# Turning x to stand by token: TensorE transposes against ScalarE block copies and VectorE 32 by 32 transposes

## The chip, the cores and the metric

The kernel runs on one core of a Trainium2 chip. The metric is the device time of one execution in microseconds (us). All arithmetic is fp32. The engines are TensorE (PE in the profile; its weight loads are PEld), VectorE (DVE), ScalarE (ACT), GpSimd (POOL) and SyncE (SP), which issues all the DMAs that matter here. Each engine runs its own instructions strictly in their order; semaphores tie the engines together.

## The reference

One layer over 2048 tokens with 1024 channels. The input is normalized per token (layernorm); the result is the input, plus a Mamba-2 block of the normalized input, plus a LoRA mixture of experts of the normalized input. Cut to the part around the change:

```
proj = hidden @ in_proj_w.T                  # gate (4096) | x (4096), B (1024), C (1024) | dt (64)
xBC  = silu(conv4(x, B, C))                  # a causal convolution of 4 taps per channel
dt_p = softplus(dt + dt_bias);  dA = exp(-dt_p * exp(A_log))
state_t = state_{t-1} * dA_t + (dt_p_t * x_t) outer B_t     # 64 heads of 64 channels, 128 states
y_t     = state_t . C_t + D * x_t
out     = (rmsnorm(y) * silu(gate)) @ out_proj_w.T
```

The recurrence is computed in chunks of 128 tokens. In a chunk, y is one matmul of a masked 128 by 128 matrix per head with `dt*x`, and the state takes one matmul of `decay*dt*x` with B. Both need `dt*x` with the tokens on the partitions, while the convolution leaves x with the channels on the partitions. So each chunk of x has to be turned.

## The kernel before

**Stages.** The projections of x, B and C (and two eighths of the gate) are made by products of 128-row weight tiles with 512-column operands (`pair`, L499), seven products of four matmuls for each two by two block of tiles (a Strassen scheme; `left_operands`, L462, makes its weight sums on GpSimd). Results go to DRAM as `raw`. The scan works on 32 blocks (L1056): two halves s of the tokens, eight groups g of 512 channels, and two halves of 512 tokens each. A block has four chunks of 128 tokens, so there are 128 slots in all (the two loops at L1087 and L1091). The later stages (gate, output projection) are not changed.

**One slot.** The slot of chunk c has, in program order: one product from the stream of projections; `scan_b` of chunk c (L812); a part of `scan_a` of the next chunk (L748); a second product; a part of `scan_a`; a third product (and a fourth in some slots); the last part of `scan_a`. `products` (L655) issues one product and then the steps of side work in that part's list: `conv` (L692) of the next block, layernorm steps, norm squares, weight sums.

`scan_a` has three parts. The first scans the decays on VectorE (`es`, L757). The second makes C by B and B transposed on TensorE into one PSUM bank (L765, L766), copies them out on ScalarE (`cbm`, `bt`, L769, L771), puts D times x into the PSUM bank of y (L778) and masks on VectorE (`dab`, L783). The third is where the change lies: four TensorE transposes of the chunk's x into the PSUM bank `st` (L788 to L790), eight ScalarE scalings by dt into `xdt` (L795, one for each head), and eight more by the decay into `xdd` (L803).

`scan_b` has eight matmuls of `xdt` and `dab` into y (L828), four of the state with C (`ps_e`, L834), two VectorE instructions that finish y (L841, L842), one matmul of `xdd` with `bt` for the state (`ps_st`, L846) and its addition (L856).

**What sets the order.** Nothing is ordered by hand for every instruction: a scheduler places them. Instructions that are passed to `keep_in_program_order` (all matmuls, the `xdt` and `xdd` scalings, the silus, the squares) keep their order on their engine; VectorE instructions passed to `pin` (L98) are chained; the rest is placed where the scheduler thinks it is ready. PSUM banks `aux`, `y`, `e` and `st` have one buffer each.

Of the kernel before, what the change touches and what calls it, by code (L numbers as in the profile page):

```python
# [8 lines left out]
F32 = mybir.dt.float32  # L9
# [34 lines left out]
def mamba_lora_kernel(  # L44
# [85 lines left out]
    def load_piece(s, i, tag, pool):  # L130

        t = pool.tile([P, KT, 2, Q], F32, tag=tag, name=f"piece_{s}_{i}")
        if s == 0:
            for h in range(2):
                nc.sync.dma_start(
                    t[:, 4 * h : 4 * h + 4].rearrange("p k n q -> p k (n q)"),
                    x_view[:, 4 * h : 4 * h + 4, i * 2 * Q : (i + 1) * 2 * Q],
                )
        else:
            for n in range(2):  # L140
                at = s * TS + n * TB + i * Q
                nc.sync.dma_start(t[:, :, n, :], x_view[:, :, at : at + Q])
        piece_of[s, i] = t
# [5 lines left out]
    for m in range(2):  # L149
        for k in range(2):  # L150
            what = f"a{m + 1}{k + 1}"
            first_w[what] = wp.tile([P, KH, P], F32, tag="w", name=f"{what}_x0_0")
            nc.sync.dma_start(first_w[what], w_in[32 + m, :, k * KH : (k + 1) * KH, :])
    load_piece(0, 2, "xg", p2)
    load_piece(0, 3, "xg", p2)

    wsm = lp.tile([P, KT, NSM], F32, name="wsm")
    nc.sync.dma_start(wsm, w_small)
# [17 lines left out]
    def op_tile(j, name):  # L176
        return op.tile([P, KH, TB], F32, tag=f"op{j}", name=name)

    ops_of["x", 0] = [op_tile(j, f"op_{j}_0") for j in range(7)]
    xop_d = [  # L180
        [dram.tile([P, KH, TB], F32, tag=f"xop_{s}_{j}", name=f"xop_{s}_{j}") for j in range(7)]
        for s in range(NS)
# [80 lines left out]
    def first_sums():  # L263


        b11, b21, b22, t4, t1, t2, b12 = ops_of["x", 0]
        nc.vector.tensor_tensor(t1, b12, b11, ALU.subtract)
        nc.vector.tensor_tensor(t2, b22, t1, ALU.subtract)
        nc.vector.tensor_tensor(t4, b21, t2, ALU.subtract)
        nc.vector.tensor_tensor(b12, b22, b12, ALU.subtract)  # L270
# [60 lines left out]
    def small(s, i, chunks, sm, home):  # L331
# [65 lines left out]

        for c in range(nch):
            nc.vector.tensor_tensor_scan(
                run[:, c, :], da[:, c, :], zero, 1.0, ALU.mult, ALU.add  # L400
            )


# [318 lines left out]
        yield  # L722


    mid_of = {}
    masked = []
    decay_of = {}
# [20 lines left out]
    def scan_a(s, g, half, c):  # L748

        key = s, g, half, c  # L750
        n = f"{s}_{g}_{half}_{c}"
        dab, ecp = decay_of.pop(key)
        hs = slice(g * HG, (g + 1) * HG)
        cs = slice(c * Q, (c + 1) * Q)

        es = p1.tile([P, HG, Q], F32, tag="es", name=f"es_{n}")
        ins = nc.vector.tensor_tensor_scan(  # L757
            es.rearrange("p h t -> p (h t)"), dab.rearrange("p h t -> p (h t)"), here, 0.0,
            ALU.mult, ALU.add,
        )  # L760
        pin(ins)
        yield
        xg, bc = xbc_of[s, g, half]
        psm = ps_one.tile([P, 3, Q], F32, tag="aux", name=f"ps_cb_{n}")
        mm(psm[:, 0, :], bc[:, 0, cs], bc[:, 1, cs], start=True, stop=True)  # L765
        transpose(psm[:, 1, :], bc[:, 0, cs])  # L766
        put_sums = norm_sum(psm[:, 2, 0:2]) if squares else None
        cbm = p2.tile([P, Q], F32, tag="cbm", name=f"cbm_{n}")
        nc.scalar.copy(cbm, psm[:, 0, :])  # L769
        bt = p2.tile([P, Q], F32, tag="bt", name=f"bt_{n}")  # L770
        nc.scalar.copy(bt, psm[:, 1, :])  # L771
        if put_sums:
            put_sums()

        psy = ps_one.tile([P, 4, Q], F32, tag="y", name=f"ps_y_{n}")
        for j in range(4):
            at = 4 * g + j
            nc.scalar.activation(  # L778
                psy[:, j, :], xg[:, j, cs], AF.Copy, scale=dsk[:, at : at + 1]
            )  # L780
        ms = dab
        masked[:] = [
            nc.vector.tensor_tensor(  # L783
                ms, es, cbm.unsqueeze(1).to_broadcast([P, HG, Q]), ALU.mult
            )
        ]
        yield
        pst = ps_one.tile([P, 4, Q], F32, tag="st", name=f"ps_xt_{n}")  # L788
        for j in range(4):
            transpose(pst[:, j, :], xg[:, j, cs])  # L790
        xdt = p2.tile([P, HG, HP], F32, tag="xdt", name=f"xdt_{n}")
        x_t = pst.rearrange("p j (a q) -> p (j a) q", q=HP)
        for h in range(HG):
            at = g * HG + h
            ins = nc.scalar.activation(  # L795
                xdt[:, h, :], x_t[:, h, :], AF.Copy,
                scale=dt_of[s][:, half * NQ + c, at : at + 1],
            )
            tc.keep_in_program_order(ins)

        xdd = p1.tile([P, HG, HP], F32, tag="xdd", name=f"xdd_{n}")
        for h in range(HG):
            ins = nc.scalar.activation(  # L803
                xdd[:, h, :], xdt[:, h, :], AF.Copy, scale=es[:, h, Q - 1 : Q]
            )
            tc.keep_in_program_order(ins)
        mid_of[key] = ms, ecp, bt, xdt, xdd, psy
        yield
# [149 lines left out]
    def out_sums(pool, i):  # L958

        p, q, kt = i // 8, i // 4 % 2, i % 4  # L960
        t = pool.tile([P, 7, 4, P], F32, tag="wo", name=f"wo_{i}")
        x = pool.tile([P, 7, P], F32, tag="wox", name=f"wox_{i}")

        def store(j, src):
            nc.sync.dma_start(w2_d[p][:, j, :, q, kt, :].rearrange("i c o -> c i o"), src)

        for j, (m, k) in enumerate(((0, 0), (0, 1), (1, 1), (1, 0))):
            nc.sync.dma_start(
                t[:, j].rearrange("c (m k) o -> c m k o", m=2),
                w_out[4 * p + 2 * k : 4 * p + 2 * k + 2, 2 * q + m, :, :, kt, :]  # L970
                .rearrange("k c m o -> c m k o"),
            )
        yield

        add(t[:, 5], t[:, 0], t[:, 3], ALU.subtract)
        add(t[:, 3], t[:, 3], t[:, 2], ALU.add)
        add(t[:, 4], t[:, 3], t[:, 0], ALU.subtract)
        add(t[:, 6], t[:, 1], t[:, 4], ALU.subtract)
        yield
        store(0, t[:, :, 0])  # L980
        store(1, t[:, :, 1])
        store(3, t[:, :, 3])
        yield
        t0, t1, t2, t3 = (t[:, :, k] for k in range(4))
        add_in_slot(x, t0, t2, ALU.subtract)
        add_in_slot(t2, t2, t3, ALU.add)
        add_in_slot(t0, t2, t0, ALU.subtract)
        add_in_slot(t1, t1, t0, ALU.subtract)
        yield
        store(6, x)  # L990
        store(4, t2)
        store(5, t0)
        store(2, t1)
        yield
# [3 lines left out]

    for h in range(HG):
        nc.gpsimd.tensor_copy(here[:, h * Q : (h + 1) * Q], ident)  # L1000
    zero = lp.tile([H, Q], F32, name="zero")
    nc.gpsimd.memset(zero, 0.0)

    rank = lp.tile([P, NE], F32, name="rank")
# [3 lines left out]
    nc.vector.tensor_scalar(na, na, -1.0, None, ALU.mult)  # L1008

    lns = [ln_first(i) for i in range(NQ)]  # L1010
    sm0 = p1.tile([P, 2 * NQ, NSM], F32, tag="y", name="sm_0")

    def small_first(i):
        for c in range(2 * i, 2 * i + 2):
# [46 lines left out]
    for part in range(3):  # L1061
        load_raw(*blocks[1], part)
    load_decays(*blocks[0], 1)

    ps = ps_one.tile([P, 4 * Q], F32, tag="y", name="ps_clear")
    mm(ps, ident, here[:, 0 : 4 * Q], start=True, stop=True)
# [20 lines left out]
    for b, blk in enumerate(blocks):  # L1087
# [3 lines left out]
        for c in range(NQ):  # L1091
# [34 lines left out]
            if nxt:  # L1126
# [5 lines left out]
                if c < 3:  # L1132
                    parts[1] += steps(conv_steps, 1)
                    parts[2] += steps(conv_steps, 1)

            products(1, parts[0])
            scan_b(*blk, c)
            if b == 16 and c == 1:
# [679 lines left out]
```

## Time and profile before

| what | value |
|---|---|
| median of 3 runs | 3382.65 us (3381.43 to 3383.46) |
| the profiled execution | 3379.91 us |
| its span on the core | 3378.1 us |
| TensorE busy | 3337.6 us, 99% of the span |
| VectorE busy | 2412.2 us, 71% |
| ScalarE busy | 1460.3 us, 43% |
| GpSimd busy | 688.3 us, 20% |
| first and last transposes of x (`ps_xt`) start | 174.6 and 2071.8 us |
| granted TensorE clock over the span | 0.998 |

How to read it: the profile is of one execution, whose own time (3379.91 us) is 2.74 us under the median of the runs; its span is 1.81 us shorter than its time. The page counts an engine as busy while an instruction of it is open, overlaps counted once, so instructions that overlap show a mean duration longer than their busy share. A group's row gives line, engine, operation, output and input, shape, count, busy us, mean ns of one, then the idle time of the engine just before such instructions and what ended it. In a timeline a row of several instructions gives the start of the first and the stretch to the end of the last. On TensorE an fp32 matmul shows as two records, a transpose as one.

### The profile page before, as it was taken

To read this page: it belongs to the slowest core of one execution; us is meant where nothing else is said; L and a number is where in the kernel's file an instruction comes from. 1 tells how busy PE (TensorE), PEld (TensorE's weight loads), DVE (VectorE), ACT (ScalarE), POOL (GpSimd) and SP (SyncE) were. 2 spreads that over 40 slices of the span, in tenths; PEclk is the share of its full clock that TensorE was granted. 3 is DMA by queue.
4 is the path that set the end of the run, shared out by engine and by line. 5 is a ranking of instruction groups with operands and counts; after the bars stand their busy time and mean duration, and the time that the engine had idled before them with its cause. 6 is when DMAs were issued, how large, how long until landed. Compare 5 with 4: busy or idle time off the path is not lost.

```text
span 3378.1 us, 41773 instructions
## 1 busy us (share of the span) xinstructions
PE 3337.6 (99%) x14021; PEld 2197.4 (65%) x14021; DVE 2412.2 (71%) x2745; ACT 1460.3 (43%) x4018; POOL 688.3 (20%) x483
## 2 busy tenths in 40 slices
PE   9999999999999999999999999999999899999999
PEld 8455555555555555555555555788888788888888
DVE  7478787878768787877787784577877666556654
ACT  2266666766665666565666663222222100000000
POOL 4122222222100021212121212355544100000000
PEclk9999999999999999999999999999999999999999
DMA  7556666656689989998888889578777886585644
GB/s 255 191 174 221 203 200 198 225 186 207 208 305 312 331 257 309 279 298 255 269 260 268 261 284 298 174 264 284 254 265 262 286 305 234 204 299 182 211 168 144
DMA packets 550821, 826.75 MB, mean 245 GB/s; under 512 B 36688, under 2 KB 266320, under 8 KB 547024
## 3 DMA queue, kind: packets, MB, share of 16 engines
q1 hardware_dynamic: 550608, 824.08, 74.0%
q8 instruction: 112, 1.84, 0.2%
q14 instruction: 101, 0.83, 0.1%
HBM read 564.88 MB, written 259.06 MB: 244 GB/s over the span
## 4 chain that ended last, share of the span: by engine, by line
PE 92%; DVE 3%; DMA 2%; ACT 2%; issue 1%; SPq 0%; DVEq 0%; ACTq 0%
PE ps_x_x L81 13%; PE ps_a_x L81 9%; PE ps_x_w L81 8%; PE ps_y_x L81 8%; PE ps_x_z L81 6%; PE ps_a_w L81 6%; PE ps_y_w L81 6%; PE ps_a_z L81 4%; PE ps_y_z L81 4%; PE ps_e L81 4%; PE ps_y L81 3%; PE ps_st L81 3%; PE ps_x_b L81 2%; PE ps_x_g L81 2%; PE ps_a_b L81 2%; PE ps_y_g L81 2%
## 5 line engine op out<-in xcount | busy, mean ns | idle before, releaser
L715 DVE SCALAR_TENSOR_TENSOR xg<-raw_x,cw,xg 128x512 f32<-128x512 f32 x384 | 344.6, 901 | 11.9 <-ACT xg L708 5.9
L85 POOL TENSOR_TENSOR state<-state,tot 128x512 f32<-128x512 f32 x112 | 120.7, 1078 | 1111.7 <-PE ps_e L81 1012.1
L81 PE MATMUL ps_x_w<-t,w 128*128 128x256 f32 x1344 | 304.3, 379 | 1.4 <-DVE kept L1719 0.8
L757 DVE TENSOR_TENSOR_SCAN es<-dab,here 128x1024 f32<-128x1024 f32 x128 | 296.1, 2313 | 9.1 <-ACT xdd L803 6.4
L81 PEld LDWEIGHTS ps_x_w<-t,w 128*128 128x128 f32 x1344 | 255.6, 190 | 44.3 <-issue 8.8
L803 ACT ACTIVATE xdd<-xdt,es 128x64 f32<-128x64 f32 x1024 | 262.4, 391 | 0.0
L778 ACT ACTIVATE ps_y<-xg,dsk 128x128 f32<-128x128 f32 x512 | 190.2, 371 | 164.7 <-DVE xg L842 150.6
L795 ACT ACTIVATE xdt<-ps_xt,dt 128x64 f32<-128x64 f32 x1024 | 223.8, 335 | 68.2 <-PE ps_xt L116 68.0
L841 DVE TENSOR_TENSOR ecp<-ecp,ps_e 128x512 f32<-128x512 f32 x120 | 82.2, 685 | 225.9 <-PE ps_e L81 207.7
L81 PE MATMUL ps_a_w<-q,w 128*128 128x256 f32 x896 | 202.6, 379 | 1.6 <-DMA w<-w 1.6
L1755 ACT COPY ps_x_w<-ps_a_w 128x512 f32<-128x512 f32 x28 | 16.0, 570 | 417.3 <-PE ps_a_w L81 417.3
L81 PEld LDWEIGHTS ps_a_w<-q,w 128*128 128x128 f32 x896 | 170.2, 190 | 25.1 <-DMA w<-w 2.0
L783 DVE TENSOR_TENSOR dab<-es,cbm 128x1024 f32<-128x1024 f32 x128 | 161.1, 1258 | 30.1 <-ACT cbm L769 29.6
L81 PEld LDWEIGHTS ps_y<-dab,xdt 128*64 128x64 f32 x2048 | 111.3, 136 | 103.5 <-ACT xdd L803 90.1
L81 PE MATMUL ps_x_x<-op_again,s_x 128*128 128x512 f32 x384 | 173.8, 595 | 0.7 <-ACT s_x L531 0.7
L81 PE MATMUL ps_a_x<-op_again,a_x 128*128 128x512 f32 x384 | 173.2, 594 | 0.0
L81 PE MATMUL ps_y_x<-op_again,s_x 128*128 128x512 f32 x384 | 173.1, 593 | 0.0
L715 DVE SCALAR_TENSOR_TENSOR bc<-raw_b,cw,bc 128x512 f32<-128x512 f32 x192 | 159.1, 830 | 18.5 <-ACT bc L708 14.6
L81 PE MATMUL ps_x_x<-op,s_x 128*128 128x512 f32 x368 | 166.2, 594 | 0.5 <-ACT s_x L531 0.5
L81 PE MATMUL ps_y_x<-op,s_x 128*128 128x512 f32 x368 | 165.9, 593 | 0.0
L81 PE MATMUL ps_a_x<-op,a_x 128*128 128x512 f32 x368 | 165.8, 593 | 0.0
L476 POOL TENSOR_TENSOR s_x<-a_x,a_x 128x512 f32<-128x512 f32 x48 | 74.8, 1559 | 362.1 <-PE ps_y_x L81 227.5
(327 smaller groups left out, 6631.8 us busy)
## 6 DMA issues: line engine op xcount, KB each, us to landing
w<-w SPq DMA_DIRECT2D x196, 512.0 KB, 3.9
dab<-da_d SPq DMA_DIRECT2D x128, 512.0 KB, 6.0
raw<-ev SPq DMA_DIRECT2D x192, 256.0 KB, 3.7
a_x<-in_w_in_dram SPq DMA_DIRECT2D x168, 256.0 KB, 4.5
w<-wo SPq DMA_DIRECT2D x96, 448.0 KB, 5.0
ecp<-run_d SPq DMA_DIRECT2D x256, 128.0 KB, 5.0
y<-xg SPq DMA_DIRECT2D x64, 512.0 KB, 5.5
gy<-y SPq DMA_DIRECT2D x64, 512.0 KB, 6.6
```

The costliest lines, as they stand in the source:

```text
L81: tc.keep_in_program_order(nc.tensor.matmul(*args, **kw))
L85: ins = nc.gpsimd.tensor_tensor(*args)
L476: nc.gpsimd.tensor_tensor(t[what], t[x], t[y], alu)
L715: ins = nc.vector.scalar_tensor_tensor(dst[:, i, :], raw[:, i, k : k + TB], cw[:, ti, k : k + 1], dst[:, i, :], ALU.mult, ALU.add,)
L757: ins = nc.vector.tensor_tensor_scan(es.rearrange("p h t -> p (h t)"), dab.rearrange("p h t -> p (h t)"), here, 0.0, ALU.mult, ALU.add,)
L778: nc.scalar.activation(psy[:, j, :], xg[:, j, cs], AF.Copy, scale=dsk[:, at : at + 1])
L783: nc.vector.tensor_tensor(ms, es, cbm.unsqueeze(1).to_broadcast([P, HG, Q]), ALU.mult)
L795: ins = nc.scalar.activation(xdt[:, h, :], x_t[:, h, :], AF.Copy, scale=dt_of[s][:, half * NQ + c, at : at + 1],)
L803: ins = nc.scalar.activation(xdd[:, h, :], xdt[:, h, :], AF.Copy, scale=es[:, h, Q - 1 : Q])
L841: pin(nc.vector.tensor_tensor(ecp, ecp, pse, ALU.mult))
L1755: nc.scalar.copy(px, pa)
```

## The change

x of a block is turned by a new generator `turned`, for two chunks (256 tokens) at a time. Sixteen ScalarE copies move 32-partition runs: run i of the channels, token block b goes to the partitions of run b, at place i (256 elements on 32 partitions each). Then one VectorE transpose of 128 by 1024 elements turns every 32 by 32 block in place. The result `x_by_token` holds two chunks and is read by the `xdt` scalings from SBUF, where they read PSUM before. The four TensorE transposes of each chunk are gone. The copies are kept in program order, the VectorE transpose is in the pinned chain. In the loop, the steps of `turned` are laid into the parts of the slots: ten in the slots of c = 2 and c = 0, seven in those of c = 3 and c = 1, the last of the seven being the transpose; the first seventeen steps of block 0 stand ahead of the loop.

The other edits: the pieces 2 and 3 of the input at the start lie in the places of two operand tiles, which are made only in `first_sums`; the early small projections (`sm0`) take a buffer of `xg`; the constant zero of a scan is one column, broadcast; and `out_sums` makes its differences in place, in another order, without the tile `wox`.

```diff
-    load_piece(0, 2, "xg", p2)
-    load_piece(0, 3, "xg", p2)
+    load_piece(0, 2, "op3", op)
+    load_piece(0, 3, "op4", op)
...
-    ops_of["x", 0] = [op_tile(j, f"op_{j}_0") for j in range(7)]
+    ops_of["x", 0] = [None if j in (3, 4) else op_tile(j, f"op_{j}_0") for j in range(7)]
...
     def first_sums():
+        for j in (3, 4):
+            ops_of["x", 0][j] = op_tile(j, f"op_{j}_0")
...
-                run[:, c, :], da[:, c, :], zero, 1.0, ALU.mult, ALU.add
+                run[:, c, :], da[:, c, :], zero.to_broadcast([H, Q]), 1.0, ALU.mult, ALU.add
...
+    by_token = {}
+
+    def turned(s, g, half):
+
+        if not by_token:
+            by_token["x"] = p1.tile([P, 2, 4 * P], F32, tag="xT", name="x_by_token")
+            by_token["in"] = p1.tile([P, 2, 4, 4, 32], F32, tag="xin", name="x_blocks")
+        xT, blocks = by_token["x"], by_token["in"]
+        x = xbc_of[s, g, half][0].rearrange("p j (c b r) -> p j c b r", c=NQ, b=4)
+        for k in range(2):
+            for i in range(4):
+                for b in range(4):
+                    ins = nc.scalar.copy(
+                        blocks[32 * b : 32 * b + 32, :, :, i, :].rearrange("p c j r -> p j c r"),
+                        x[32 * i : 32 * i + 32, :, 2 * k : 2 * k + 2, b, :],
+                    )
+                    tc.keep_in_program_order(ins)
+                    yield
+            ins = nc.vector.transpose(
+                xT.rearrange("p c x -> p (c x)"),
+                blocks.rearrange("p c j i r -> p (c j i r)"),
+            )
+            pin(ins)
+            yield
...
-        pst = ps_one.tile([P, 4, Q], F32, tag="st", name=f"ps_xt_{n}")
-        for j in range(4):
-            transpose(pst[:, j, :], xg[:, j, cs])
         xdt = p2.tile([P, HG, HP], F32, tag="xdt", name=f"xdt_{n}")
-        x_t = pst.rearrange("p j (a q) -> p (j a) q", q=HP)
+        x_t = by_token["x"][:, c % 2, :].rearrange("p (h q) -> p h q", q=HP)
...
-        x = pool.tile([P, 7, P], F32, tag="wox", name=f"wox_{i}")
...
-        add_in_slot(x, t0, t2, ALU.subtract)
-        add_in_slot(t2, t2, t3, ALU.add)
-        add_in_slot(t0, t2, t0, ALU.subtract)
+        add_in_slot(t3, t2, t3, ALU.add)
+        add_in_slot(t2, t0, t2, ALU.subtract)
+        add_in_slot(t0, t3, t0, ALU.subtract)
         add_in_slot(t1, t1, t0, ALU.subtract)
         yield
-        store(6, x)
-        store(4, t2)
+        store(6, t2)
+        store(4, t3)
...
-    zero = lp.tile([H, Q], F32, name="zero")
+    zero = lp.tile([H, 1], F32, name="zero")
...
-    sm0 = p1.tile([P, 2 * NQ, NSM], F32, tag="y", name="sm_0")
+    sm0 = p2.tile([P, 2 * NQ, NSM], F32, tag="xg", name="sm_0")
...
     load_decays(*blocks[0], 1)
+    turn = turned(*blocks[0])
+    for _ in range(17):
+        next(turn)
...
+            if c == 2 and nxt:
+                turn = turned(*nxt)
+            if c < 2 or nxt:
+                for p, k in zip(parts, ((2, 3, 3, 2), (3, 4), (0, 3, 4, 3), (3, 4))[c]):
+                    p += steps(turn, k)
```

## The prediction

> **What bounds the kernel now.** I read the page's busy shares first, then the stretch of the scan by windows, then the groups by shape, TensorE's waits, and one slot's timeline.
>
> ```profile
> PE 3337.6 (99%) x14021; PEld 2197.4 (65%) x14021; DVE 2412.2 (71%) x2745; ACT 1460.3 (43%) x4018; POOL 688.3 (20%) x483
> ```
> ```profile
> 200.00:2000.00 1800.00, 1786.82 (x7314) 952.17 (x7313) 1424.52 (x1719) 1138.18 (x3401) 348.72 (x250) 1.00 0.79 251
> ```
>
> The second line is the scan stage (PE, PEld, DVE, ACT, POOL). TensorE is the bound there, idle for 13 of 1800 us at full clock; VectorE is busy 79% and ScalarE 63%. Some 123 of the 128 slots lie in it, so a slot lasts 14.7 us, of which ScalarE works 9.3 and VectorE 11.6.
>
> ```profile
> L116 PE MATMUL ps_xt<-ident,xg 128*128 128x128 f32 x512 | 76.8, 273 | 0.0
> ```
> ```profile
> L803 ACT ACTIVATE xdd<-xdt,es 128x64 f32<-128x64 f32 x1024 | 262.4, 391 | 0.0
> L795 ACT ACTIVATE xdt<-ps_xt,dt 128x64 f32<-128x64 f32 x1024 | 223.8, 335 | 68.2 <-PE ps_xt L116 68.0
> ```
> ```profile
> L757 DVE TENSOR_TENSOR_SCAN es<-dab,here 128x1024 f32<-128x1024 f32 x128 | 296.1, 2313 | 9.1 <-ACT xdd L803 6.4 <-DMA raw<-ev 2.4 <-DMA dab<-da_d 0.4
> L783 DVE TENSOR_TENSOR dab<-es,cbm 128x1024 f32<-128x1024 f32 x128 | 161.1, 1258 | 30.1 <-ACT cbm L769 29.6
> ```
> ```profile
> PE ps_st L81 <- ACT xdd L803: 4.8, 10, 1.4
> ...
> PE ps_y L81 <- ACT xdt L795: 4.6, 3, 1.6
> ```
>
> The first is what goes. The next two are the ScalarE scalings that use its result; the two after are the VectorE rows nearest to the new transpose. The last two are TensorE's waits for the scalings: small today. How much room there is behind them is the question, and one slot's timeline shows it, TensorE first, then ScalarE:
>
> ```profile
> 729.33 0.60 PE L116 MATMUL ps_xt<-ident,xg 128*128 128x128 f32 x4
> 729.77 3.60 PE L81 MATMUL ps_y_g<-op,s_g 128*128 128x512 f32 x8
> 733.30 1.09 PE L81 MATMUL ps_y<-dab,xdt 128*64 128x128 f32 x16
> 734.32 1.16 PE L81 MATMUL ps_e<-bc,state 128*128 128x128 f32 x8
> 735.32 1.02 PE L81 MATMUL ps_st<-xdd,bt 128*128 128x512 f32 x2
> ```
> ```profile
> 726.26 0.26 ACT L769 COPY cbm<-ps_cb 128x128 f32<-128x128 f32 x1
> 726.40 0.28 ACT L771 COPY bt<-ps_cb 128x128 f32<-128x128 f32 x1
> 729.53 0.57 ACT L523 COPY ps_x_g<-ps_a_g 128x512 f32<-128x512 f32 x1 [2.84 <-PE ps_a_g L81]
> 730.01 1.06 ACT L879 ACTIVATE sq<-xg 128x1024 f32<-128x1024 f32 x1
> 730.97 1.75 ACT L795 ACTIVATE xdt<-ps_xt,dt 128x64 f32<-128x64 f32 x8
> 732.55 2.05 ACT L803 ACTIVATE xdd<-xdt,es 128x64 f32<-128x64 f32 x8
> ```
>
> Here xdd ends at 734.60 and `ps_st`, which needs all of it, starts at 735.32: 0.7 us to spare with a square (0.96) ahead of xdt, about 1.7 without.
>
> **What goes.** The four transposes start at 729.33 and the next product at 729.77: 0.44 us for four, 0.11 each, though each row says 273 ns (they overlap). 128 slots make **-56 us**, all on the path, since TensorE is never ahead of its inputs for long.
>
> The Trainium skill ("VectorE: DVE Perf Modes", The three transpose paths and Rules for kernel authors) speaks against this change: it would have a full 128 by 128 transposed on TensorE, VectorE's being blocks of 32 only. But it puts TensorE's at 390 ns each (bf16); by that 512 would give back an estimated 200 us, and the sum would be clearly faster. The trace's pace of 0.11 us decides.
>
> **What ScalarE takes on.** 32 copies for each of 32 blocks, 1024 of 256 elements from SBUF. No such row stands in the trace. Start to start, a copy of 128 columns takes 0.14 us (726.26 to 726.40), one of 512 takes 0.48 (729.53 to 730.01): 0.25 at 256 on that line, from PSUM. From SBUF the square of 1024 takes 0.96 (730.01 to 730.97), which less 768 columns at the same slope (0.34/384) is 0.28. The far end is xdd, 64 columns from SBUF in 0.24, plus 192 at that slope: 0.41, but with a scale read from memory, which a copy lacks. So between 0.25 and 0.41; I take **0.31**, near the copies. Eight per slot are 2.5 us. xdt now reads SBUF, so it paces like xdd: 8 x (0.238 - 0.197) = 0.3 us. ScalarE's slot grows from 9.3 to 12.1 of about 14.5 us (at 0.41: 12.9). It isn't full, but its queue is in order, so what counts is where the copies stand.
>
> **What lies on the path.** xdt used to wait for `ps_xt`, right behind the second product, with one product (3.43 us) left before `ps_y`. In the built order of the changed kernel xdt needs nothing fresh from TensorE, but it stands behind ScalarE copies of product results (s5, s16, ev), which wait for that same second product, and in 42 of the 128 slots five or more block copies stand between the two. Such a slot, from the end of the product: 0.2 to start, 0.49 for the result copy, 7 x 0.31 = 2.2 for the block copies, 8 x 0.24 = 1.9 for xdt, 1.9 for xdd, 0.1 at the end: 6.8 us. TensorE meanwhile has the product 3.43, `ps_y` 1.03, `ps_e` 1.0: 5.46. It waits about **1.3 us**. The same count over all slots (rows' paces, the actual gate in each):
>
> - 22 slots with seven copies behind the gate, mostly 1.3: 26 us
> - 13 with five, mostly 0.6: 9 us
> - 7 with eight, ten or fourteen: 9 us
> - the other 86: mostly nothing; 18 us from a few with layernorm or table work in the queue
>
> Together **+62 us** at 0.31; the same count gives +46 at 0.25 and +93 at 0.41. For the kernel before, this count gives 2 us, where the trace has TensorE waiting 10.7 for these scalings, so it errs low if anywhere.
>
> **The start.** The first turn stands ahead of the loop. ScalarE's copy of a product result at 173.6 (the end of TensorE's last product) comes first in the built order, then 16 copies (5.0), the VectorE transpose (1.25), xdt and xdd. Today `ps_y` starts at 178.5 there. It would start about **6 us** later; 5 to 8 over the bounds.
>
> **VectorE.** 64 transposes of 128x1024. Nearest rows: L783 at 1.26 and the scan L757 at 2.31; I take 1.25, since it reads one input and feeds nothing back, and 0.62 (half of L783) as the lower end. 0.5 per slot is +0.6 us, to 12.2 of 14.5 us. `dab`, the VectorE result that TensorE needs, is done in the median slot 4.7 us before `ps_y` (the trace, slot by slot), and in ten slots under 1.2 us. Put at 0 to 3 us; I take 0, hidden by that slack. If it were gone, up to 64 x 1.25 = 80 us.
>
> **Edits with one answer, nothing.** `first_sums` now overwrites pieces 2 and 3: its first subtraction runs at 66.0, the last product that reads them ends at 62.5. `sm0` in a buffer of `xg` is read out long before block 1's convolution wants it. `out_sums` in place has the same four instructions; the first waits for a store issued over a slot earlier (these land in 3 to 12 us). One column of zeros changes no row (L399, 16 x 0.39). The DMAs stay the same in number. Each, if its cover failed, costs a few us once, `out_sums` a few us in each of 16 slots.
>
> **Sum.** -56 + 62 + 6 = **+12 us** against the profiled execution's 3379.9, so 3392; that one ran 2.7 below the median, so **3395** against 3382.65. At 0.25: -56 + 46 + 5 = -5; at 0.41: -56 + 93 + 8 = +45. The break-even pace is 0.27.
>
> **Rivals.**
> - *The gates don't bite (not slower).* Place: the copies between a result copy and xdt. Price: below 0.27 us a copy the gain wins. If 32 partitions or plain copies pace at 0.20, the count gives 33 + 4, so -19: 3363; with no waits at all 3327. For it: the 128-column copies at 0.14, ScalarE's 37% idle. Against: SBUF sources pace slower, and 42 slots have the copies behind the gate.
> - *Dear copies.* Strided runs of 32 elements moved between partitions are in no row; at 0.41 the time is 3428, and ScalarE is so full that delays run into the next slot. For it: xdd's pace. Against: no pointer to read.
> - *VectorE becomes the bound.* At 2.31 per transpose its slot reaches 12.8 of 14.5 us; the in-order wait of the transpose for the last copy then holds `dab` behind it, 0.6 us in each of 64 slots: 38 more, 3433. For it: ten slots have under 1.2 us of slack. Against: the median has 4.7.
>
> **How the numbers follow.** Forecast 48% (3380 to 3415), gates don't bite 20%, dear copies 20%, VectorE 12%. A time within 0.2% (6.8 us, about what can be told from no change) reaches from 3376 to 3389. Faster: the second case and a little of the first, 0.22. Same: the low part of the first, 0.20. Slower: 0.58. The range takes in 0.25, 0.41 and VectorE's case, and most of the 0.20 case: 3355 to 3440. The full gain of 3327 and copies above 0.45 us are left out.
>
> **What would show it.** Right: `ps_xt` gone from TensorE; its busy time down by about 56 us or more and its idle time in the scan up from 13 to about 75 us, the waits put down to ACT xdt and xdd; copies starting 0.31 us apart; `ps_y` first starting near 184. Wrong: copies 0.25 apart or less, TensorE still 99% busy there, or its waits put down to DVE `dab`.

## The result, and the profile after

The changed kernel takes **3460.32 us** (median of 4 runs, 3457.09 to 3461.15) against 3383.06 for the kernel before (4 runs): a ratio of 1.0227, 95% interval 1.0209 to 1.0245. That is 77 us slower, where 12 were forecast; the range ended at 3440. The profiled execution took 3461.15 us, its span 3459.4 us at a granted clock of 0.996.

The page's busy line of the changed kernel, and its scan stretch by windows (PE, PEld, DVE, ACT, POOL busy, then clock, DMA share, GB/s):

```profile
PE 3351.5 (97%) x13509; PEld 2184.1 (63%) x13509; DVE 2486.9 (72%) x2809; ACT 1904.0 (55%) x5038; POOL 688.8 (20%) x483
```
```profile
200.00:2000.00 1800.00, 1730.24 (x6576) 905.41 (x6576) 1439.15 (x1719) 1495.55 (x4192) 336.62 (x239) 1.00 0.76 241
```

TensorE has 512 transposes fewer, yet it is busy 14 us *longer*. In the scan it now idles 70 us of 1800, where it idled 13, and ScalarE went from 1138 to 1496 busy. The `ps_y` matmuls of the last slot start at 2156.5 us in place of 2075.4: 81 us later, as much as the two profiled spans differ. What follows takes as long as before (1303 us to the end of the span, both times), so the loss is all in the scan and its start.

The groups that answer to those shown of before, from the groups by shape of the changed kernel:

```profile
L739 ACT COPY x_blocks<-xg 32x256 f32<-32x256 f32 x1024 | 411.5, 402 | 14.0
L819 ACT ACTIVATE xdt<-x_by_token,dt 128x64 f32<-128x64 f32 x1024 | 258.8, 335 | 50.2 <-DVE x_by_token L745 49.3
L81 PE MATMUL ps_y<-dab,xdt 128*64 128x128 f32 x2048 | 186.1, 289 | 41.9 <-ACT xdt L819 32.5 <-DVE dab L810 9.0 <-PE ps_a_x L81 0.4
L745 DVE STREAM_TRANSPOSE x_by_token<-x_blocks 128x1024 f32<-128x1024 f32 x64 | 79.2, 1238 | 67.1 <-ACT x_blocks L739 67.0
```

The first row is the block copies: mean 402 ns, and busy 411.5 us for 1024, which is 0.40 each. Mean times count equals busy, so no two overlap; compare xdt, whose mean of 335 ns times 1024 is 343 us against 259 busy. The last row: the VectorE transpose takes 1.24 us, as assumed, but now someone waits for it (the 49.3 us in the second row). The third row tells most of why TensorE's busy time rose. Before, it read:

```profile
L81 PE MATMUL ps_y<-dab,xdt 128*64 128x128 f32 x2048 | 142.4, 279 | 5.9 <-ACT xdt L795 4.6 <-ACT xdd L803 1.3
```

The group went from 142 to 186 us busy, though one matmul is hardly longer (289 ns against 279). They now start further apart, at the pace at which xdt delivers its heads; and as each record is open for some 0.28 us, the next one starts before it ends, so the small waits between them don't show as idle time. A wait can hide in a busy time.

TensorE's waits for the two scalings, in the changed kernel (us in total, times, longest):

```profile
PE ps_y L81 <- ACT xdt L819: 32.5, 42, 3.5
PE ps_st L81 <- ACT xdd L827: 28.8, 63, 1.5
PE ps_y L81 <- DVE dab L810: 9.0, 2, 7.5
```

Before, these waits were 4.6 and 4.8. One slot of the changed kernel shows how they come about, ScalarE first, then TensorE:

```profile
744.30 0.28 ACT L378 ACTIVATE tot<-ps_tot 128x128 f32<-128x128 f32 x1 [1.12 <-PE ps_tot L116]
...
744.85 2.89 ACT L739 COPY x_blocks<-xg 32x256 f32<-32x256 f32 x7
747.75 2.02 ACT L819 ACTIVATE xdt<-x_by_token,dt 128x64 f32<-128x64 f32 x8
749.68 2.00 ACT L827 ACTIVATE xdd<-xdt,es 128x64 f32<-128x64 f32 x8
```
```profile
744.10 3.60 PE L81 MATMUL ps_y_x<-op,s_x 128*128 128x512 f32 x8
748.15 2.10 PE L81 MATMUL ps_y<-dab,xdt 128*64 128x128 f32 x16 [0.45 <-ACT xdt L819]
```

ScalarE idles until TensorE releases it at 744.30 (here by `ps_tot`, a small matmul beside the products), then does two small instructions, seven copies and xdt. TensorE is ready for `ps_y` at 747.70, 3.4 us after that point, and waits; the sixteen `ps_y` matmuls then take 2.10 us in place of 1.09, at the pace of xdt. This is the mechanism of the forecast, with copies at 0.41 us start to start.

The waits have a price that the forecast's sum had no term for: the granted clock. Up to the last `ps_y`, the trace before shows the full clock throughout; that of the changed kernel shows 0.5 in four spells of 3.4 or 6.8 us, 20.5 us in all. One of them:

```profile
560.54 2.36 PE L81 MATMUL ps_y<-dab,xdt 128*64 128x128 f32 x16 [1.90 <-ACT xdt L819]
562.83 2.05 PE L81 MATMUL ps_e<-bc,state 128*128 128x128 f32 x8
```
```profile
561.30:564.70 3.40, 3.40 (x21) 3.07 (x20) 0.00 (x0) 3.38 (x14) 0.00 (x0) 0.50 0.65 236
```

The eight `ps_e` matmuls take 2.05 us here and 1.16 in the slot shown of before. Half of TensorE's busy time inside the four spells, an estimate of what they cost, is 8 us of the 77.

### The profile page after: what moved, and what is told of

Same layout as the page of the kernel before. It is cut to its first block, busy times and chain, and to the rows that moved or that the text cites. A ratio compares the mean times of both kernels' runs of the same rounds, so it can differ in the third digit from the quotient of the medians.

```text
span 3459.4 us, 41787 instructions
## 1 busy us (share of the span) xinstructions
PE 3351.5 (97%) x13509; PEld 2184.1 (63%) x13509; DVE 2486.9 (72%) x2809; ACT 1904.0 (55%) x5038; POOL 688.8 (20%) x483
## 4 chain that ended last, share of the span: by engine, by line
PE 65%; ACT 18%; DVE 11%; DMA 3%; issue 3%; POOL 0%; SPq 0%; DVEq 0%; ACTq 0%; POOLq 0%
PE ps_x_w L81 8%; PE ps_x_x L81 8%; PE ps_x_z L81 6%; PE ps_a_w L81 5%; PE ps_y_w L81 5%; PE ps_y_x L81 5%; PE ps_a_x L81 5%; ACT x_blocks L739 5%; PE ps_a_z L81 4%; PE ps_y_z L81 4%; ACT xdt L819 4%; ACT xdd L827 4%; DVE xg L717 3%; PE ps_st L81 3%; PE ps_x_b L81 2%
## 5 line engine op out<-in xcount | busy, mean ns | idle before, releaser
L739 ACT COPY x_blocks<-xg 32x256 f32<-32x256 f32 x1024 | 411.5, 402 | 14.0
L819 ACT ACTIVATE xdt<-x_by_token,dt 128x64 f32<-128x64 f32 x1024 | 258.8, 335 | 50.2 <-DVE x_by_token L745 49.3
L81 PEld LDWEIGHTS ps_y<-dab,xdt 128*64 128x64 f32 x2048 | 141.2, 137 | 155.8 <-ACT xdt L819 115.6
L81 PE MATMUL ps_y<-dab,xdt 128*64 128x128 f32 x2048 | 186.1, 289 | 41.9 <-ACT xdt L819 32.5
```

The lines of the kernel that those rows point to most:

```text
L81: tc.keep_in_program_order(nc.tensor.matmul(*args, **kw))
L739: ins = nc.scalar.copy(blocks[32 * b : 32 * b + 32, :, :, i, :].rearrange("p c j r -> p j c r"), x[32 * i : 32 * i + 32, :, 2 * k : 2 * k ...
L819: ins = nc.scalar.activation(xdt[:, h, :], x_t[:, h, :], AF.Copy, scale=dt_of[s][:, half * NQ + c, at : at + 1],)
```

## The experiments

**Theory:** the loss is waiting. It comes from block copies that stand, in ScalarE's queue, between a gated result copy and xdt, at 0.41 us each, and from xdt waiting for VectorE transposes that come late in VectorE's queue. **Rivals:** ScalarE's load, wherever the copies stand; VectorE's load; xdt's new source; a side edit. The halved clock is no rival of its own, since it came with the waits, but it makes some of them dearer. All differences below are against the kernel before as run beside each experiment (3378.7 to 3381.4 us).

### Why the copies do not overlap: two runs of copies alone

Copies back to back between tiles in SBUF (the lines are shortened), where `to(t, b, i)` is the change's destination and `frm(i, b)` its source; the group `f` moves the change's runs of 32 elements on all 128 partitions, eight copies in the same 2.54 us as the flat `e`:

```diff
+        a: for i, for b: nc.scalar.copy(to(a, b, i), frm(i, b))
+        b: for i, for b: nc.scalar.copy(to(t, b, i), frm(b, i))
+        c: for i:        nc.scalar.copy(to(t, 0, i), frm(0, i))
+        d: for i, for b: nc.scalar.copy(t[32 * b : 32 * b + 32, i, :], x[32 * i : 32 * i + 32, b, 0:256])
+        e: for i < 8:    nc.scalar.copy(t[:, i, :], x[:, i // 2, ...])
```

> Computes nothing of the reference: it runs groups of 4 to 16 ScalarE copies of 256 float32 elements back to back, with nothing to wait for, and then two groups on VectorE. In the changed kernel a block copy takes 0.40 us and the next starts 0.41 us later, so two never overlap, while PSUM copies over all 128 partitions do. Three readings of why: (1) the move to other partitions (source run and destination run differ): then the same copies inside one run of partitions pace at 0.31 or less, and the flat ones that shift stay at 0.41; (2) only 32 partitions, or a destination run that changes from copy to copy: then copies inside their own run, run after run, are as slow as the shifted ones, and those that stay in one run are faster; (3) the pattern of runs of 32 elements: then flat copies are at 0.31 or less, shifted or not, and strided ones over all 128 partitions are at 0.41. Copies of 512 elements, if nothing overlaps, would take about 0.40 + 0.21 = 0.61 to 0.62 us. VectorE's copies of the same blocks are in no row so far: 0.2 to 0.4 us.

The timeline of ScalarE in that run (start, stretch of the whole group, the copies in it):

```profile
7.19 6.60 ACT L32 COPY a_shift<-x 32x256 f32<-32x256 f32 x16
13.82 6.60 ACT L36 COPY b_same_runs<-x 32x256 f32<-32x256 f32 x16
20.44 1.32 ACT L39 COPY c_one_run<-x 32x256 f32<-32x256 f32 x4
...
22.89 6.60 ACT L46 COPY d_flat_shift<-x 32x256 f32<-32x256 f32 x16
...
31.95 2.54 ACT L54 COPY f_runs_all<-x 128x256 f32<-128x256 f32 x8
```

A single copy of 256 takes 0.40 us in every group. Sixteen in 6.60 are (6.60 - 0.40) / 15 = 0.413 apart; four in 1.32 are 0.307 apart, eight in 2.54 are 0.306. Neither the shift to other partitions, nor the runs of 32 elements, nor the 32 partitions alone cost the overlap: `c` has 32 partitions and keeps it, `b` does not shift and loses it. What `a`, `b` and `d` share is that the run of partitions changes from one copy to the next.

```diff
+        p: for b, for i: nc.scalar.copy(to(t, b, i), frm(i, b))
+        q: for i, for b: nc.scalar.copy(to(t, b, i), frm(i, b))
+        r: for i:        nc.scalar.copy(to(t, 1, i), frm(0, i))
+        t: for i < 8:    nc.scalar.copy(t[0:64, i, :], x[0:64, i // 2, ...])
+        u: for i < 8:    d = 64 * (i % 2); nc.scalar.copy(t[d : d + 64, i, :], x[64 - d : 128 - d, i // 2, 0:256])
```

> Computes nothing of the reference: back-to-back groups of ScalarE copies of 256 float32 elements, as in the first such run, where a copy took 0.40 us in every group, but the next started 0.31 us later if both stayed on the same partitions (128 of them, or one run of 32) and 0.41 us later if the run of partitions changed from one copy to the next, shifted or not, flat or strided. Which change costs the overlap? If it is that of the destination run: with the loops exchanged (all four sources into one destination run, then the next run) 12 of 16 starts are 0.31 apart, some 5.4 us for 16 against 6.6. If any change of either run costs it: 6.6 us again, and only the groups with both runs fixed have 0.31, also when source and destination differ. Copies of 64 partitions that alternate between halves: 0.41; in one half: 0.31. The same copies on GpSimd are in no row: 0.3 to 1.5 us each.

The groups that decide, from the timeline of ScalarE in that run:

```profile
13.83 6.60 ACT L36 COPY p_dst_fixed<-x 32x256 f32<-32x256 f32 x16
20.45 6.61 ACT L40 COPY q_src_fixed<-x 32x256 f32<-32x256 f32 x16
27.06 1.32 ACT L43 COPY r_both_fixed_shift<-x 32x256 f32<-32x256 f32 x4
...
29.72 2.54 ACT L49 COPY t<-x 64x256 f32<-64x256 f32 x8
32.28 3.30 ACT L53 COPY u_shift<-x 64x256 f32<-64x256 f32 x8
```

A change of either run, source or destination, costs the overlap; with both fixed it is there, shifted or not (`r`). So no order of the sixteen copies of a block wins it back: each has its own pair of runs. The forecast's 0.31 was the right pace for copies that stay where they are, and the wrong one for these.

The Trainium skill ("ScalarE: Activation LUTs", What ACT_TABLE_LOAD costs) states, for an instruction whose scale and bias are constants, a fixed part and a part by element that make an estimated 399 ns for 256 elements, and an overlap of about 93 ns between neighbours, by which the pace would be an estimated 306 ns. Both agree with the groups that stay on their partitions (400 and 306 ns); the overlap is absent where the run changes (413 ns).

### Neither, one, or both: the cost of copies and transposes

Without the block copies (the tile cleared once):

```diff
-                    ins = nc.scalar.copy(
-                        blocks[32 * b : 32 * b + 32, :, :, i, :].rearrange("p c j r -> p j c r"),
-                        x[32 * i : 32 * i + 32, :, 2 * k : 2 * k + 2, b, :],
-                    )
-                    tc.keep_in_program_order(ins)
```

> The change without its 1024 block copies: the tile that they fill is cleared once, so the values of x that enter the scan are left out. VectorE transposes, xdt from SBUF, and every side edit stay. Theory (the block copies in front of xdt and xdd make TensorE wait): the 56 us of transposes are won and little is lost, 3327 to 3345 us. Rival, VectorE's transposes or the dearer reading of xdt from SBUF cost the time: 3400 us or more. Rival, the side edits cost it: 3440 or more.

Measured 3367.48, -13 us (ratio 0.9966, 0.9954 to 0.9978). Neither side's number: the copies are most of the loss, but the gain is 43 us short of the full 56. The wait that remains, from ScalarE's waits in that run:

```profile
ACT xdt L815 <- DVE x_by_token L741: 58.9, 24, 6.8
```

xdt waits 24 times for a transpose, although nothing holds the transpose up but its place in VectorE's queue: in all 24 cases it follows other VectorE work without a pause, in 21 of them a step of the convolution. So the transposes go too:

```diff
-            ins = nc.vector.transpose(...)
-            pin(ins)
```

> The change without its block copies and without its VectorE transposes: x_by_token is cleared once, so the values of x that enter the scan are left out; xdt reads it from SBUF, and every side edit stays. Without the copies alone the time was 3367 us, 13 below the kernel before, where 50 had been expected. Theory (there xdt waits for the VectorE transposes, which come late in VectorE's queue): without them the whole 56 us are won, 3323 to 3335. Rivals, the SBUF source of xdt or a side edit takes the 40 us: 3360 to 3370.

Measured 3337.07, -42 us (0.9872, 0.9858 to 0.9887): a little above the theory's 3335, far from the rivals. The transposes alone cost 28 us. What is missing to 56 could lie in the side edits, so these were run by themselves: no copies, no VectorE transposes, and TensorE's transposes kept in these two places:

```diff
         pst = ps_one.tile([P, 4, Q], F32, tag="st", name=f"ps_xt_{n}")
         for j in range(4):
             transpose(pst[:, j, :], xg[:, j, cs])
...
         x_t = pst.rearrange("p j (a q) -> p (j a) q", q=HP)
```

> Computes the reference. The kernel before with the change's side edits alone (pieces 2 and 3 in operand tiles, sm0 in a buffer of xg, the broadcast zero, the differences in place); TensorE's transposes are kept, there are no copies and no VectorE transposes; the change's two tiles are set aside, one of them cleared once. Without copies and transposes the change gained 42 us where 56 had been expected. If the side edits cost nothing, as predicted: 3378 to 3384, and the missing 14 us are waits that come out once TensorE is 0.44 us a slot shorter. If they cost the 14: 3390 to 3396.

Measured 3380.11, 0.9996 (0.9987 to 1.0006): nothing, as predicted. The last corner, copies without VectorE transposes:

```diff
-        x_t = by_token["x"][:, c % 2, :].rearrange("p (h q) -> p h q", q=HP)
+        x_t = by_token["in"][:, c % 2].rearrange("p j i r -> p (j i r)").rearrange("p (h q) -> p h q", q=HP)
```

> The change without its VectorE transposes: xdt reads the copied blocks as they stand, so each 32 by 32 block enters the scan unturned. With this run all four cases of copies and transposes are there: neither 3337, transposes alone 3367, both 3460. If the two costs simply add, the copies alone take 93 us: 3425 to 3435. If each makes the other dearer (the transpose waits for the last copy and holds VectorE's queue, xdt then waits for the transpose): below 3415. If the copies alone already give the whole loss, as a load on ScalarE that no order changes: 3445 or more.

Measured 3441.10, +61 us (1.0177, 1.0162 to 1.0192), a little above the additive range. Against the kernel before:

| | no VectorE transposes | with them |
|---|---|---|
| no copies | -42 | -13 |
| copies | +61 | +77 |

The copies cost 103 us without transposes and 90 with them, the transposes 28 and 16. They nearly add; each covers some 12 us of the other. (The +77 is against the kernel before as run beside the change.)

The copies added to the kernel before (the last kernel with side edits alone, and these lines of `turned`; nobody reads the copies):

```diff
+                    ins = nc.scalar.copy(
+                        blocks[32 * b : 32 * b + 32, :, :, i, :].rearrange("p c j r -> p j c r"),
+                        x[32 * i : 32 * i + 32, :, 2 * k : 2 * k + 2, b, :],
+                    )
+                    tc.keep_in_program_order(ins)
```

> The kernel before (TensorE's transposes kept, xdt read from PSUM, the reference computed in full) with the side edits and the 1024 block copies added at the change's places, into a tile that nothing reads; no VectorE transposes. Theory: the count of waits at the measured 0.41 us a copy, 93 us, on top of the kernel before, and some more where they delay the next slot: 3465 to 3495. If the copies cost little by themselves and xdt's new inputs are what is dear: 3385 to 3400.

Measured 3448.51, +68 us (1.0207, 1.0192 to 1.0222), below the theory's 3465. The comparison is telling: taking TensorE's transposes out gains 40 us where there are no copies (-1 to -42) and 7 where there are (+68 to +61). In a slot that waits for ScalarE, a shorter TensorE waits longer: of the 1800 us from 200 to 2000, TensorE idles 32 with the transposes and the copies and 58 with the copies alone. So what a term costs depends on the order in which they are counted. Added to the kernel before, the copies cost 69 us, and the removal then brings 7.

### Is it the pace?

All copies on one run of partitions:

```diff
-                        blocks[32 * b : 32 * b + 32, :, :, i, :].rearrange("p c j r -> p j c r"),
-                        x[32 * i : 32 * i + 32, :, 2 * k : 2 * k + 2, b, :],
+                        blocks[0:32, :, :, i, :].rearrange("p c j r -> p j c r"),
+                        x[0:32, :, 2 * k : 2 * k + 2, b, :],
```

> The change with its 1024 copies in the same places and number, but all of them from partitions 0 to 31 to partitions 0 to 31, so that consecutive ones stay on one run and start 0.31 us apart in place of 0.41; the other 96 partitions of the tile are cleared once, so three quarters of x that enter the scan are left out. It tells what the missing overlap cost by itself. By the count of the waits, 93 us at 0.41 and 62 at 0.31, 31 us less than the change, up to 50 with less backlog: 3410 to 3430. If the pace hardly matters (the mere presence of the copies, or the transposes, cost the time): 3445 or more.

Measured 3454.45, +73 us (1.0220, 1.0203 to 1.0237): as the rival had it, though ScalarE's busy time in the scan's 1800 us fell from 1496 to 1408. But the expectation's "same places" did not hold: the scheduler laid the other ScalarE work differently between these copies, and 466 of them came to stand between the last product's result copy and xdt, where the change has 427. With two things changed, the run gives no price of the pace; that the shorter copies won so little in it is not explained. The next leaves runs and places and halves each copy:

```diff
-                        blocks[32 * b : 32 * b + 32, :, :, i, :].rearrange("p c j r -> p j c r"),
-                        x[32 * i : 32 * i + 32, :, 2 * k : 2 * k + 2, b, :],
+                        blocks[32 * b : 32 * b + 32, 0:1, :, i, :].rearrange("p c j r -> p j c r"),
+                        x[32 * i : 32 * i + 32, :, 2 * k : 2 * k + 1, b, :],
```

> The change with copies of 128 elements in place of 256, the other half of the tile cleared once, so half of x that enters the scan is left out. Number, runs of partitions and places stay (437 copies between the last product's result copy and xdt in place of 427; in the run with all copies on one run of partitions it was 466, and the scheduler had interleaved them otherwise, so that run did not settle the price of the pace). By the lengths of 256 and 512 elements (0.402 and 0.614 us) such a copy takes 0.30 and starts 0.31 after the last: the pace that the prediction had assumed. If its size was what failed, the count of the waits falls by 31 to 36 us: 3422 to 3432. If the presence of the copies rather than their pace costs (each slot then waits for something else that is late): 3445 or more.

The copies' group of that run, then its time:

```profile
L740 ACT COPY x_blocks<-xg 32x128 f32<-32x128 f32 x1024 | 302.1, 295 | 13.8
```

Measured 3431.37, +51 us (1.0153, 1.0136 to 1.0170). With the assumed price per copy the time falls by 26 us, near the 31 to 36 of the count. So the pace is one mis-sized term, and not the only one: at 0.31 the change is still 51 slower, not 12. (Shorter copies lighten ScalarE's load too, which this run doesn't tell from the pace.)

### Is it the place?

The same copies spread over the first two products of a slot:

```diff
-                for p, k in zip(parts, ((2, 3, 3, 2), (3, 4), (0, 3, 4, 3), (3, 4))[c]):
+                for p, k in zip(parts, ((4, 5, 0, 0), (3, 5), (3, 6, 0, 0), (3, 5))[c]):
```

> The change with the same 1024 copies and 64 transposes, spread over the first two products of each slot ((4, 5, 0, 0), (3, 5), (3, 6, 0, 0), (3, 5) steps in place of (2, 3, 3, 2), (3, 4), (0, 3, 4, 3), (3, 4)), so that in no slot a block copy stands between the last product's result copy and xdt. ScalarE has exactly as much to do as in the change. Theory (the place behind the last gate is what costs): most of the wait goes, but not that for the VectorE transposes in every second slot, 20 to 30 us, and the start's 7: 3350 to 3370 us, faster than before. Rival (ScalarE's load, wherever it stands, is what costs): 3445 to 3465, as the change.

Measured 3409.22, +29 us (1.0091, 1.0074 to 1.0108): 49 of the 77 us go with the place, ScalarE's load unchanged. The expectation's "in no slot" held only in the main. By the trace, 31 copies in 11 slots still stand between ScalarE's last copy of a TensorE result and xdt, where the change has 283 in 62 slots; counted from the last product's result copy, as above, 192 are left. The theory's 3350 to 3370 is missed all the same; xdt still waits for the transposes about as long as in the change:

```profile
ACT xdt L819 <- DVE x_by_token L745: 47.7, 22, 6.1
```

An attempt to move everything earlier, the transpose by a product, xdt and xdd to stand behind cbm:

```diff
+                for p, k in zip(parts, ((4, 6, 0, 0), (7, 0), (4, 6, 0, 0), (7, 0))[c]):
...
-        yield
         xdt = p2.tile([P, HG, HP], F32, tag="xdt", name=f"xdt_{n}")
```

> Computes the reference. The same copies and transposes as the change, spread as (4, 6, 0, 0), (7, 0), (4, 6, 0, 0), (7, 0) over the products of a slot, so that the VectorE transpose is issued one product earlier, and xdt and xdd are issued right behind cbm, two products before ps_y in place of one. Theory (what stands late in the two queues costs the time, not the load): the waits for xdt, xdd and the transposes nearly vanish, 3335 to 3355 us, some waits of products for their result copies may appear in their place. Rival (ScalarE's load): 3400 or more, as 3409 in the run with the copies spread.

Measured 3434.88, +56 us (1.0158, 1.0141 to 1.0175): wrong, and worse than the run before. VectorE's waits in it name the reason:

```profile
DVE x_by_token L745 <- ACT x_blocks L739: 217.4, 58, 9.8
```

The transpose now stood right behind the copies it needs; VectorE came to it before they were done, in 58 of 64 cases, and everything behind it waited. Part of TensorE's waits moved to results of the products (11.0 us for `ev`, 9.8 for `s_x`). So the transpose has to be early in VectorE's queue and the copies earlier still:

```diff
+                for p, k in zip(parts, ((4, 6, 0, 0), (6,), (4, 6, 0, 0), (6,))[c]):
+                    p += steps(turn, k)
+                if c in (1, 3):
+                    parts[1][:0] = steps(turn, 1)
```

> Computes the reference. Copies on ScalarE as in the change, all of them one product earlier than where they were spread before ((4, 6, 0, 0), (6), (4, 6, 0, 0), (6) over the products of a slot), and the VectorE transpose first among the second product's side work in place of last, ahead of two convolution steps. Theory (what is left of the loss at 3409 is half the transposes coming late in VectorE's queue, 30 us, half copies): 3380 to 3400. If the load of ScalarE sets the rest: 3405 or more.

Measured 3393.38, +12 us (1.0038, 1.0023 to 1.0053), as the theory had it. The same two waits in this run:

```profile
DVE x_by_token L745 <- ACT x_blocks L739: 10.8, 3, 9.8
```
```profile
ACT xdt L819 <- DVE x_by_token L745: 8.9, 7, 2.9
```

Both all but gone, with VectorE's load as before. 65 of the 77 us were a matter of where the same instructions stand. Against the run with neither copies nor transposes (-42) it is still 54 us dearer: its `ps_y` starts 9 us late, an estimated 12 us go to the halved clock, and TensorE waits 37 us for xdt and xdd, the late start among them (11 in the kernel before).

### Is it the load as well?

The copies on GpSimd, at the change's places:

```diff
-                    ins = nc.scalar.copy(
+                    ins = nc.gpsimd.tensor_copy(
```

> Computes the reference. The change with its block copies on GpSimd, at the same places in the program; GpSimd is busy 20% and took 0.39 us for such a copy when it had nothing else to do, 400 us in all. ScalarE is rid of them. Theory (the copies in ScalarE's queue ahead of xdt): as without copies, 3367, and up to 7 us for the start: 3362 to 3380, no slower than the kernel before. Rival: GpSimd's copies come late or slow VectorE, and the transposes wait for them: 3395 or more.

Measured 3468.86, +88 us (1.0260, 1.0245 to 1.0275): the rival. The group of the copies, by shape, and ScalarE's wait:

```profile
L739 POOL COPY x_blocks<-xg 32x256 f32<-32x256 f32 x1024 | 757.7, 740 | 117.4 <-DVE x_by_token L745 62.3 <-ACT xg L707 7.1 <-DMA state<-st 5.7
```
```profile
ACT xdt L819 <- DVE x_by_token L745: 127.4, 35, 12.4
```

A copy that took 392 ns alone takes 740 here, so the turn is late and xdt waits for it. This run's trace tells when. The 206 copies that met no VectorE instruction took 0.39 us, and so did 103 beside sums of which one input lies in PSUM (`state`, and `xg` from `ps_y`); 104 beside the convolution of `bc`, whose two inputs lie in SBUF, took 0.76 (the median), and 86 beside the scan `es` took 2.3, about as long as that scan. The long waits of xdt bring the halved clock too: 0.985 over the span, by the same estimate 36 of the 88 us. The same in the better order (this edit and the last one before it together):

> Computes the reference. Both of the last two: copies on GpSimd and spread earlier, the VectorE transpose first among the second product's side work. Theory: neither ScalarE's copies nor late transposes hold xdt up, as in the run without both (3337), and 7 us for the start: 3340 to 3358, faster than the kernel before. Rival, contention of GpSimd with VectorE: 3380 or more.

Measured 3394.43, +13 us (1.0039, 1.0024 to 1.0054): the rival again, and close to the run with ScalarE's copies. Last, that order with every second copy on each engine:

```diff
-                    ins = nc.scalar.copy(
+                    move = nc.gpsimd.tensor_copy if b % 2 else nc.scalar.copy
+                    ins = move(
```

> Computes the reference. As in the run with the transpose first and the copies a product earlier (3393 us), with every second copy on GpSimd (0.70 us each there beside VectorE's work, 358 us in all) and the others on ScalarE (210 us). Neither queue is then as full as when it had all the copies (3393 and 3394): 3368 to 3385 if the load of each queue is what is left; 3390 or more if it is the order, the start and the transposes.

Measured **3374.56**, -6 us (0.9979, 0.9970 to 0.9989). Its scan by windows:

```profile
200.00:2000.00 1800.00, 1764.02 (x6887) 920.88 (x6886) 1528.54 (x1794) 1366.03 (x3910) 717.75 (x734) 1.00 0.79 252
```

This version is 0.2% faster than the kernel before. TensorE idles 36 us of the 1800, where it idled 70 in the change and 47 with this order and all copies on ScalarE; ScalarE is busy 1366, against 1496 and 1540. So the rival of load is right for a part: with the order cured, splitting the load wins another 18 us (+12 to -6).

## Why the prediction was wrong

The sign was right, and so was the place where most of the loss arises, copies behind a gate on ScalarE and xdt behind them. Three terms of the sum were mis-sized, all toward too little, and two costs were in no term: the halved clock, and what a fuller ScalarE queue costs where no gate stands.

- **What goes, -56, "all on the path".** Measured alone it is -42, and with the copies there only -7. The side edits cost nothing, as predicted, so the other 14 belong to the removal itself and to xdt's source. With TensorE 0.44 us a slot shorter, small waits of some slots may come out that it had covered; this was not taken apart.
- **The copies, +62 at 0.31.** The two bounds were 0.25 and 0.41, and the far one, xdd's pace, is what the trace shows: 0.41. The step that failed first is the choice of the near row: the 128-column copies that overlap do so on all partitions, the block copies change theirs each time. At 0.41 the prediction's count gave 93, with the start's 8 together 101; the copies measured 103 by themselves. That the two agree so closely is in part luck. With most copies moved off the last gate, 49 of the 77 us went, not all; at the assumed pace the count, with the measured -42 and 16, makes -42 + 62 + 6 + 16 = 42, and the run was at 51. What the count leaves out is the load and the clock.
- **VectorE, "0 to 3; I take 0, hidden by that slack".** It cost 28 us alone and 16 beside the copies. The duration was right (1.24 for 1.25). What failed is the place that was looked at: the slack of `dab` was weighed, but the new wait is that of xdt for the transpose, which stands in VectorE's order behind the convolution steps of the same part. The prediction had named no queue in front of the transpose.
- **The start, +6, `ps_y` near 184:** it starts at 185.5 in place of 178.5, 7 us. The number was right, the end of the path was not (the two rows below): VectorE stood until the sixteen copies were done, and behind the transpose came the scan `es` and `dab`. `dab` released `ps_y`, while the first head of xdt was done at 183.85.
- **Sum:** -42 + 103 + 16 = +77, the start within the 103; the forecast had -56 + 62 + 0 + 6.

```profile
180.62 1.25 DVE L745 STREAM_TRANSPOSE x_by_token<-x_blocks 128x1024 f32<-128x1024 f32 x1 [9.85 <-ACT x_blocks L739]
```
```profile
185.51 1.97 PE L81 MATMUL ps_y<-dab,xdt 128*64 128x128 f32 x16 [7.47 <-DVE dab L810]
```

Of the rivals, *dear copies* was the one that came: its 3428 had the pace right and lacks the transposes and the 14 us. *VectorE becomes the bound* did not come as priced; the transpose cost by its place, not by its length, and its wait held up a `dab` that TensorE needed at the start. *The gates don't bite* is refuted: no block copy of the change paced below 0.27, and moving them off the gates won 49 us.

Of what would show it: the scan's idle time rose to 70 us where 75 was said, and the waits were put down to xdt and xdd; but the 75 belonged to a sum of +12. That TensorE's busy time would fall by 56 us was wrong: it rose by 14, with 44 us more in the `ps_y` group alone. Idle and busy have to be read together where records overlap.

## What to carry to other kernels

Work that is moved off the busiest engine is paid at its place in the other engine's in-order queue: count what stands between the last gated instruction there and the consumer, and do it for every engine that the new chain runs through, a transpose on VectorE as well as the copies ahead of it. Price an instruction by a row that changes its partitions in the same way, not only one of the same size, and keep the far bound where no such row exists. Where such a change loses, try the order before giving up the change: here the order brought back 65 of 77 us, and a split of the load made it 0.2% faster than before.

## What the runs showed of the hardware

- In these runs two neighbouring ScalarE copies overlap by 0.09 to 0.10 us only if source and destination each stay on their run of partitions: 0.306 us apart against 0.413 for 256 elements, with 32 as with 64 partitions, shifted or not.
- A copy of 256 elements takes ScalarE the same 0.40 us on 32 partitions as on 128, and one of 512 elements 0.61; VectorE took 0.28 for 32 by 256 (the runs of copies alone).
- A GpSimd copy of 32 by 256 took 0.39 us by itself and 0.74 in the scan: 0.39 with VectorE idle, 0.76 beside its convolution of `bc`, 2.3 beside the scan `es`. The Trainium skill ("GPSIMD Engine Reference", 1. Specifications) says that GpSimd shares its SBUF interfaces with VectorE and contends with VectorE instructions that run in a 2-port mode or have two SBUF inputs. This trace agrees for the second: `bc` and `es` have two, and beside sums with one input in PSUM a copy took 0.39.
- After some of TensorE's longer waits the granted clock stood at 0.5 for 3.4 or 6.8 us, and matmuls in that time took about twice as long (`ps_e` 2.05 us in place of 1.16).
